# First modulation as rows, and the way in around it, in an adaLN block with random-feature attention and a routed feed-forward

## Chip, cores and metric

The kernel runs on one core of one Trainium2 chip. The metric is device time in microseconds (us) of one execution. All data is fp32.

## What is computed

Inputs: x (2 x 2048 x 256), a conditioning vector c (2 x 256), weights. With `_layernorm` over the 256 channels:

```python
mod = (_silu(L0_c) @ L0_wmod).reshape(2, 6, 1, 256)
sa, ca, ga, sb, cb, gb = mod[:, 0], ..., mod[:, 5]
ga = sign(ga) * max(|ga|, 0.25);  gb = sign(gb) * max(|gb|, 0.25)
h = _layernorm(x) * (1 + ca) + sa
x = x + ga * attn(h)
h = _layernorm(x) * (1 + cb) + sb
x = x + gb * ffn(h)
```

In `attn`, q, k and v come from `h @ W_attn + b_attn` with 16 heads of 16 channels; q and k are scaled by 1/4 and become 128 positive features each, `exp(x @ omega - |x|^2 / 2) / sqrt(128)`; the causal output is a running sum over keys, divided by its own normaliser, then projected. `ffn` routes each token to 2 of 4 experts that share Wi and Wo and differ by a rank-4 term. The change touches only the first modulation (sa and ca), the first layer norm's way to the attention, and the bias of q and k for the first block of tokens.

## The kernel before

**Tiling.** Each batch's 2048 tokens are cut into 4 blocks of 512, so there are 8 blocks; a block has 4 chunks of 128 tokens. Channels are split into KC = 2 halves of 128 partitions. Heads go in NG = 4 groups of HG = 4. Odd chunks are kept with their tokens reversed. The main loop runs over 8 blocks and 8 pairs of (group, two chunks), and interleaves with a block's attention the way in of the next block and the feed-forward of the ones before. At its end `keep_written_order` ties each engine's instructions to the order in which the program writes them, so each engine works its list in that order and waits only for data. The same holds for the queues: SyncE (SP) and ScalarE (ACT) each issue their DMAs in written order.

**The way in** is what runs once, before the main loop, to have block 0's features ready (lines 906 to 941, and the loads and constants from line 122 on):

- SP loads c (`ct_sb`, L122) and block 0's x in four pieces (L99). ScalarE issues the loads of `wm[0]` and `wm[1]` (the columns of wmod for sa and ca, L131), computes exp(-c) into `sig` (L135), then issues the loads of the q and k bias `bqk` (L136) and of the key and query columns of `w_sb` (L138). VectorE finishes silu(c) as `cs` (L140 to L142). SP goes on with omega (L144), the value columns (L145), the value bias (L146) and block 1's x.
- `warm(n, bank)` (L213) multiplies the identity by itself n times into a bank that nobody reads. WARM gives the counts, here 6 and 4.
- `ln_halves` (L306) computes mean and variance of the four chunks on VectorE and, by halves, the inverse root on GpSimd (L315).
- `columns(0)` (L245) computes the modulation as columns: for each of four groups of 128 outputs and each half k, the wm block is the stationary operand (128x128) and `cs`, two columns wide, is streamed. VectorE copies the result to `modT` and adds one into `scale1` (L252, L253).
- `norm1(0)` (L321) writes the normalised x, `xh`, on VectorE; `second_columns` (L171 to L175) prepares two small constants; `weights_twice` (L414) copies w_sb's query and key columns into a doubled layout `wd` on GpSimd.
- `channels1(0)` calls `to_channels`: for each half k, four transposes (L331) into one bank, then two evictions on VectorE (L342), for the even chunks and the reversed odd chunks, which apply scale1 and modT and write `hT`.
- `bias_twice` (L406, L408) doubles the bias; `twice_product` (L422) makes the doubled q and k, `pd`; VectorE adds the bias (L429), ScalarE and VectorE square every second row (L433, L441), and `features` (L476) multiplies by omega.

PSUM tiles come from rings: four banks for `mm_tile`, two for `side_tile`, and two fixed banks `pa`.

Of the kernel before, what the change touches and what calls it, by code (L numbers as in the profile page):

```python
# [9 lines left out]
FP = mybir.dt.float32  # L10
AF = mybir.ActivationFunctionType
ALU = mybir.AluOpType
AX = mybir.AxisListType

P = 128
# [17 lines left out]
def kernel(  # L33
# [18 lines left out]
    nc = tc.nc  # L52
    B, T, C = x.shape
    KC = C // P
# [6 lines left out]
    TB = 512  # L61
    NT = TB // P
# [5 lines left out]
    CG = P // 4  # L68


    W0, RHO = ER, ER + 1
    WARM = (6, 4)
    TH = TB // 2
    RG = 4
    assert M == P and KC == 2 and C == NH * DH and ER + 2 <= HW and RG * HW == P
# [1 line left out]
    const = ctx.enter_context(tc.tile_pool(name="const", bufs=1))  # L77
    work = ctx.enter_context(tc.tile_pool(name="work", bufs=2))
# [5 lines left out]
    def mm_tile(name):  # L84
        return psum.tile([P, TB], FP, tag="mm", name=name)
# [5 lines left out]
    st = {}  # L91
# [11 lines left out]
    w_sb = const.tile([P, KC, 3 * C], FP, name="w_sb")  # L103
# [3 lines left out]
    bqk = const.tile([P, 4], FP, name="bqk")  # L107
# [9 lines left out]
    modT = const.tile([P, 12, B], FP, name="modT")  # L117
    scale1 = const.tile([P, 2, KC, B], FP, name="scale1")
# [6 lines left out]
    wm = []  # L125
# [3 lines left out]
    wav = w_attn.rearrange("(k p) n -> p k n", p=P)  # L129
# [2 lines left out]

    cs = const.tile([P, KC, B], FP, name="cs")
    sig = const.tile([P, KC, B], FP, name="sig")
    nc.scalar.activation(sig, ct_sb, AF.Exp, scale=-1.0)  # L135
    nc.scalar.dma_start(bqk, b_attn[0 : 2 * C].rearrange("(c p) -> p c", p=P))  # L136
    for n in (1, 0):
        nc.scalar.dma_start(w_sb[:, :, n * C : (n + 1) * C], wav[:, :, n * C : (n + 1) * C])  # L138
    nc.vector.memset(om, -0.5)
    nc.vector.tensor_scalar_add(sig, sig, 1.0)  # L140
    nc.vector.reciprocal(sig, sig)
    nc.vector.tensor_mul(cs, ct_sb, sig)  # L142
    for j in range(HG):
        nc.sync.dma_start(om[2 * DH * j : 2 * DH * j + DH, :], omega)  # L144
    nc.sync.dma_start(w_sb[:, :, 2 * C : 3 * C], wav[:, :, 2 * C : 3 * C])  # L145
# [3 lines left out]
    ident = const.tile([P, P], FP, name="ident")  # L149
# [10 lines left out]
    def halves(ap):  # L160
        return ap.rearrange("p (j s d) -> p j s d", s=2, d=DH)
# [6 lines left out]
    def second_columns():  # L168

        second_row = work.tile([P, P], FP, tag="kt", name="second_row", bufs=1)  # L170
        nc.vector.memset(halves(second_row[:])[:, :, 0, :], 0.0)  # L171
        nc.vector.memset(halves(second_row[:])[:, :, 1, :], 1.0)
        nc.vector.tensor_mul(second_row, second_row, ident)
        nc.vector.tensor_reduce(on_second[:, 0:1], second_row, AX.X, ALU.add)
        nc.vector.tensor_scalar(on_second[:, 1:2], on_second[:, 0:1], -1.0, 1.0, ALU.mult, ALU.add)  # L175
# [6 lines left out]
    pa = [psum.tile([P, TB], FP, tag=f"pa{n}", name=f"pa{n}", bufs=1) for n in range(2)]  # L182
# [27 lines left out]
    def warm(n, bank):  # L210

        for _ in range(n):
            nc.tensor.matmul(bank[:, 0:P], ident, ident, start=True, stop=True)  # L213
# [25 lines left out]
    def columns(which):  # L239

        pm = mm_tile(f"pm{which}")
        pmv = pm[:, 0 : 4 * B].rearrange("p (n b) -> p n b", b=B)
        for n in range(4):
            for k in range(KC):
                nc.tensor.matmul(  # L245
                    pmv[:, n, :],
                    wm[3 * which + n // 2][:, k, (n % 2) * P : (n % 2 + 1) * P],
                    cs[:, k, :],
                    start=(k == 0),
                    stop=(k == KC - 1),  # L250
                )
        nc.vector.tensor_copy(modT[:, 6 * which : 6 * which + 4, :], pmv)  # L252
        nc.vector.tensor_scalar_add(  # L253
            scale1[:, which], modT[:, 6 * which + 2 : 6 * which + 4, :], 1.0
        )

    def gate(b, gi):

        pg = mm_tile(f"pg{b}_{gi}")
        for k in range(KC):  # L260
            nc.tensor.matmul(
                pg[:, 0:C], csb[b][:, k, :], wm[2 + 3 * gi][:, k, :],
                start=(k == 0), stop=(k == KC - 1),
            )
        gt2 = work.tile([P, 2, C], FP, tag="rho", name=f"gate{b}_{gi}", bufs=1)
        sgn, row = gt2[:, 0, :], gt2[:, 1, :]
        nc.vector.tensor_scalar(sgn, pg[:, 0:C], 0.0, 2.0, ALU.is_ge, ALU.mult)
        nc.vector.tensor_scalar_add(sgn, sgn, -1.0)
        nc.vector.tensor_mul(row, pg[:, 0:C], sgn)
        nc.vector.scalar_tensor_tensor(row, row, 0.25, sgn, ALU.max, ALU.mult)  # L270
        if gi == 0:
            nc.vector.tensor_mul(
                wp_g[b], wp_g[b], row.unsqueeze(1).to_broadcast([P, KC, C])
            )
            nc.vector.tensor_mul(bp_g[b], bp_g[b], row)
        else:
            rows_g[b] = row
# [18 lines left out]
    def ln_chunk(src, stats, mv, t):  # L296
        nc.vector.bn_stats(stats[:, t, :], src[:, t, :])
        nc.vector.bn_aggr(mv[:, t, :], stats[:, t, :])
# [4 lines left out]
        nc.gpsimd.tensor_tensor(rstd, rstd, mhalf, ALU.pow)  # L303
        return mv, rstd

    def ln_halves(src, nm):  # L306

        stats = work.tile([P, NT, 6], FP, tag="stats", name=f"stats{nm}")
        mv = work.tile([P, NT, 2], FP, tag="mv", name=f"mv{nm}")
        rstd = work.tile([P, NT], FP, tag="rstd", name=f"rstd{nm}")  # L310
        for h in (slice(0, 2), slice(2, 4)):
            for t in range(h.start, h.stop):
                ln_chunk(src, stats, mv, t)
            nc.vector.tensor_scalar_add(rstd[:, h], mv[:, h, 1], LN_EPS)
            nc.gpsimd.tensor_tensor(rstd[:, h], rstd[:, h], mhalf[:, h], ALU.pow)  # L315
        return mv, rstd

    def ln_apply(src, mv, rstd, nm):
        xh = work.tile([P, NT, C], FP, tag="xh", name=f"xh{nm}", bufs=1)
        for t in range(NT):  # L320
            nc.vector.tensor_scalar(  # L321
                xh[:, t, :], src[:, t, :], mv[:, t, 0:1], rstd[:, t : t + 1],
                ALU.subtract, ALU.mult,
            )
        return xh

    def to_channels(src, dst, b, which, nm, tiles):
        for k in range(KC):
            pt = tiles[k](f"pt{nm}_{k}")
            for t in range(NT):  # L330
                nc.tensor.transpose(  # L331
                    pt[:, t * P : (t + 1) * P], src[:, t, k * P : (k + 1) * P], ident
                )

            parts = ((0, 1), (1, -1)) if which == 0 else ((None, 1),)
            for odd, step in parts:
                out, ins = (
                    ap if odd is None else
                    ap.rearrange("p (a o u) -> p a o u", o=2, u=P)[:, :, odd, :]
                    for ap in (dst[:, k, :], pt[:])  # L340
                )
                nc.vector.tensor_scalar(  # L342
                    out if step > 0 else out[:, :, ::-1], ins,
                    scale1[:, which, k, b : b + 1],
                    modT[:, 6 * which + k, b : b + 1],
                    ALU.mult, ALU.add,
                )
# [15 lines left out]
    def norm1(i):  # L363
        s = st[i]
        s["xh"] = ln_apply(s["x"], *s["ln"], f"a{i}")
# [8 lines left out]
    def channels1(i, *tiles):  # L374
        s = st[i]
        s["hT"] = work.tile([P, KC, TB], FP, tag="hT", name=f"hT{i}", bufs=1)
        to_channels(s["xh"], s["hT"], i // NBLK, 0, f"a{i}", tiles or (side_tile, side_tile))
        s["feat"], s["qd"] = {}, {}
# [24 lines left out]
    def bias_twice():  # L403
        pb = mm_tile("pb")
        for g in range(2):
            nc.tensor.matmul(pb[:, 4 * g : 4 * g + 4], dup[:, g, :], bqk, start=True, stop=True)  # L406
        st["bias"] = const.tile([P, 2, 4], FP, name="bias_twice")
        nc.vector.tensor_copy(st["bias"], pb[:, 0:8].rearrange("p (g n) -> p g n", n=4))  # L408

    def weights_twice(g, side, tag):  # L410
        wd = work.tile([P, KC, P], FP, tag=tag, name=f"wd{g}{side}", bufs=2 if tag == "y" else 1)
# [283 lines left out]
    def norm2(i):  # L695
        st[i]["xh"] = ln_apply(st[i]["x"], *st[i]["ln"], f"f{i}")
# [207 lines left out]


    warm(WARM[0], pa[0])
    st[0]["ln"] = ln_halves(st[0]["x"], "a0")
    columns(0)
    warm(WARM[1], pa[1])
    norm1(0)  # L910
    second_columns()
    for g, side, tag in ((0, 1, "y"), (0, 0, "y"), (1, 1, "lT0"), (1, 0, "lT1")):
        weights_twice(g, side, tag)
    channels1(0)
    bias_twice()
    twice_product(0, 1, "qs", mm_tile)
    twice_product(0, 0, "qs", mm_tile)
    squares_under(0, 1)
# [172 lines left out]
    for i in range(N):  # L1091
        for k in range(PAIRS):
            n = (i * PAIRS + k) * 2
            g, t = k // 2, 2 * (k % 2)
# [46 lines left out]
    p, q = N - 1, N - 2  # L1141
# [97 lines left out]
```

## Time and profile before

| | us |
|---|---|
| three runs | 757.05, 759.88, 760.32 (median 759.88) |
| the profiled execution | 756.79 |
| its span, first to last instruction | 755.0 |
| first TensorE instruction (L213) | 1.43 |
| `columns(0)`, 16 instructions (L245) | 4.46 to 8.04 |
| first instruction of pd (L422) | 12.08 |
| first exp of the main work (L487) | 19.03 |

A matmul of fp32 data stands as two instructions in the profile, a transpose as one. PE is TensorE's matmuls, PEld its weight loads, DVE is VectorE, ACT ScalarE, POOL GpSimd, SP SyncE. In the timeline a row gives the start and the length in us, the engine, the line, what is written and read, the shapes, how many instructions were merged, and in brackets how long the engine had been idle and what ended it. In the chain of waits, each piece is what the last instruction of the span had to wait for, followed back; it gives the start, the length and the work.

### The profile page before, as it was taken

Reading aid. Unit: us, or ns where it says so; the run is one execution under the profiler, and the core shown is the slowest. Engines: PE = TensorE matmul, PEld = TensorE weight load, DVE = VectorE, ACT = ScalarE, POOL = GpSimd, SP = SyncE. Lnnn points to the kernel's source line nnn. Section 1 sums busy time; section 2 is a strip of 40 time slices with the busy share of each in tenths; the row PEclk is TensorE's granted clock in tenths of the full one; section 3 lists DMA queues with packets and bytes.
Section 4 is the critical chain, followed back from the end, with each engine's and each line's share of the span. In section 5 each row is a group of like instructions: output and inputs, shape, how many; then the busy total and the mean of one; then the engine's idle time right before and its main releaser. Section 6 shows DMA issues by size and latency. Waiting matters only on the chain.

```text
span 755.0 us, 24542 instructions
## 1 busy us (share of the span) xinstructions
PE 744.8 (99%) x10720; PEld 552.1 (73%) x10720; DVE 407.0 (54%) x1133; ACT 329.6 (44%) x742; POOL 148.3 (20%) x192
## 2 busy tenths in 40 slices
PE   9999999999999999999999999999999999999998
PEld 6667776666787767776787677877688777777776
DVE  5667667564663547534656456645364424654612
ACT  1665546535544444435544455435454343521010
POOL 3000322222210322011220122103130112005122
PEclk9999999999999999999999999999999999999999
DMA  4369443123301433023420342204240130002000
GB/s 134 111 195 298 146 143 100 44 82 120 114 29 32 129 112 114 17 72 119 124 72 33 111 125 82 67 29 130 73 127 16 50 110 17 16 34 83 1 29 28
DMA packets 44234, 65.46 MB, mean 87 GB/s; under 512 B 6752, under 2 KB 20256, under 8 KB 44128
## 3 DMA queue, kind: packets, MB, share of 16 engines
q1 hardware_dynamic: 42240, 62.33, 26.1%
q8 instruction: 84, 1.38, 0.8%
q10 hardware_dynamic: 1888, 1.58, 0.7%
q14 instruction: 22, 0.18, 0.1%
HBM read 35.32 MB, written 28.57 MB: 85 GB/s over the span
## 4 chain that ended last, share of the span: by engine, by line
PE 93%; DVE 4%; ACT 1%; issue 1%; DMA 0%; POOL 0%; DVEq 0%
PE ph L836 13%; PE pf L874 12%; PE pa L552 9%; PE pp L476 9%; PE pq L384 7%; PE ph L821 4%; PE pk L500 4%; PE pv L457 4%; PE py L621 4%; PE py L576 4%; PE py L627 3%; PE po L682 3%; PE pt L597 3%; PE pf L896 2%; PE ph L522 2%; PE pta L331 1%
## 5 line engine op out<-in xcount | busy, mean ns | idle before, releaser
L865 POOL TENSOR_TENSOR g<-g,r 128x256 f32<-128x256 f32 x128 | 90.6, 741 | 416.3 <-DVE r L864 416.3
L487 ACT ACTIVATE phi<-pp,lnm 128x512 f32<-128x512 f32 x256 | 155.2, 689 | 9.7 <-PE pp L476 3.6
L874 PE MATMUL pf<-wo_g,g 128*128 128x256 f32 x448 | 103.6, 382 | 0.4 <-ACT phi L487 0.2
L836 PE MATMUL ph<-h,wi_sb 128*128 128x256 f32 x448 | 101.9, 380 | 0.1
L836 PEld LDWEIGHTS ph<-h,wi_sb 128*128 128x128 f32 x448 | 84.3, 190 | 12.5 <-DVE r L864 0.5
L874 PEld LDWEIGHTS pf<-wo_g,g 128*128 128x128 f32 x448 | 82.6, 190 | 13.7 <-issue 2.2
L552 PEld LDWEIGHTS pa<-phi,phi 128*32 128x32 f32 x4096 | 77.5, 110 | 14.8 <-issue 13.3
L552 PE MATMUL pa<-phi,phi 128*32 128x128 f32 (+3 forms) x4096 | 85.4, 235 | 0.1
L850 ACT ACTIVATE g<-ph 128x256 f32<-128x256 f32 x112 | 33.9, 389 | 115.1 <-PE ph L821 115.1
L635 ACT COPY y<-py 128x128 f32<-128x128 f32 x128 | 27.8, 269 | 125.2 <-DVE ds L588 123.4
L561 DVE TENSOR_TENSOR am<-pa,causal 128x512 f32<-128x512 f32 x128 | 81.8, 681 | 0.0
L391 DVE TENSOR_SCALAR qs<-pq,bqk 128x512 f32<-128x512 f32 x30 | 22.5, 751 | 99.3 <-PE pq L384 94.6
L476 PE MATMUL pp<-f,om 32*128 32x512 f32 x512 | 73.6, 640 | 0.0
L542 ACT COPY kt<-pk 128x512 f32<-128x512 f32 x82 | 44.5, 594 | 54.8 <-PE pk L500 54.7
L864 DVE SCALAR_TENSOR_TENSOR r<-ph,rho 128x256 f32<-128x256 f32 x112 | 41.7, 422 | 45.6 <-PE ph L821 23.2
L384 PE MATMUL pq<-hT,w_sb 128*128 128x512 f32 x120 | 58.5, 612 | 0.0
L588 DVE COPY ds<-py 128x256 f32<-128x256 f32 (+1 forms) x63 | 25.7, 407 | 52.6 <-PE py L627 47.0
L621 PE MATMUL py<-am,v 128*32 128x128 f32 x1024 | 51.4, 273 | 0.0
L627 PE MATMUL py<-phi,S 128*32 128x128 f32 x960 | 50.1, 273 | 0.0
L597 PEld LDWEIGHTS pt<-ident,ds 128*128 128x128 f32 x120 | 12.8, 140 | 44.6 <-DVE ds L588 38.7
L500 PE MATMUL pk<-ident,phi 128*128 128x128 f32 x328 | 44.9, 275 | 0.5 <-ACT phi L487 0.4
L500 PEld LDWEIGHTS pk<-ident,phi 128*128 128x128 f32 x328 | 37.7, 141 | 7.1 <-ACT phi L487 3.0
(159 smaller groups left out, 968.2 us busy)
## 6 DMA issues: line engine op xcount, KB each, us to landing
f<-qd SPq DMA_DIRECT2D x60, 256.0 KB
qd<-qs SPq DMA_DIRECT2D x58, 256.0 KB
ydr<-y SPq DMA_DIRECT2D x32, 256.0 KB
num<-ydr SPq DMA_DIRECT2D x16, 256.0 KB
inv<-rdr SPq DMA_DIRECT2D x16, 256.0 KB
xt<-in_x_dram SPq DMA_DIRECT2D x7, 512.0 KB
out_dram<-xt SPq DMA_DIRECT2D x7, 512.0 KB
wo_g<-in_woT_dram SPq DMA_DIRECT2D x2, 1024.0 KB
```

Of the source, the lines that this page charges most:

```text
L384: nc.tensor.matmul(pq, w_sb[:, k, n * P : (n + 1) * P], s["hT"][:, k, :], start=(k == 0), stop=(k == KC - 1),)
L476: nc.tensor.matmul(pp, om[rs, :], f[rs, :], start=True, stop=True, tile_position=(2 * DH * j, 0))
L487: nc.scalar.activation(ph, pps[j], AF.Exp, bias=lnm)
L500: nc.tensor.transpose(pk[:, j * P : (j + 1) * P], phi[i, g, 1, j][:, t * P : (t + 1) * P], ident)
L542: nc.scalar.copy(kt.rearrange("p h m -> p (h m)"), turned[i, g, t])
L552: nc.tensor.matmul(pa[t % 2][c * CG : (c + 1) * CG, j * P + q0 : j * P + q1], phi[i, g, 1, j][:, t0 + c * CG : t0 + (c + 1) * CG], phi[i, ...
L561: nc.vector.tensor_mul(am, pa[t % 2][:].rearrange("p (h q) -> p h q", h=HG), causal[t % 2][:].unsqueeze(1).to_broadcast([P, HG, P]),)
L621: nc.tensor.matmul(py[rows[j], :], v[:, t, g * HG + j, :], am[:, j, :], start=True, stop=state is None,)
L627: nc.tensor.matmul(py[rows[j], :], state[:, rows[j]], phi[i, g, 0, j][:, tok], start=False, stop=True,)
L836: nc.tensor.matmul(ph, wi_sb[:, k, f * P : (f + 1) * P], s["h2"][:, k, ts], start=(k == 0), stop=False, skip_group_check=True,)
L865: nc.gpsimd.tensor_add(g, g, r)
L874: nc.tensor.matmul(po, s["g"][f][:, t * P : (t + 1) * P], wo_g[i // NBLK][:, f, :], start=(f == 0), stop=(f == NF - 1), skip_group_check=True,
```

## The change

The modulation for sa and ca is computed as rows: silu(c), repeated to 32 columns (`cs_rows`), is the stationary operand, the wm blocks are streamed 128 columns at a time into four groups of 32 partitions, ScalarE copies the result to SBUF, one transpose makes columns of it, and ScalarE writes modT and scale1 from there. `ln_halves` takes two functions that are called after its two halves, and the modulation, identity products and `bias_twice` stand there; the bias copy moves to ScalarE. The first block's transposes go chunk by chunk into four banks, and two of the four evictions are ScalarE's. `second_columns` moves behind them. There are four runs of identity products (7, 5, 8, 4) where there were two (6, 4). ScalarE issues the key columns' load before its exp, and bqk's load goes to SP, ahead of omega.

```diff
-    WARM = (6, 4)
+    WARM = (7, 5, 8, 4)
...
+    nc.scalar.dma_start(w_sb[:, :, C : 2 * C], wav[:, :, C : 2 * C])
     nc.scalar.activation(sig, ct_sb, AF.Exp, scale=-1.0)
-    nc.scalar.dma_start(bqk, b_attn[0 : 2 * C].rearrange("(c p) -> p c", p=P))
-    for n in (1, 0):
-        nc.scalar.dma_start(w_sb[:, :, n * C : (n + 1) * C], wav[:, :, n * C : (n + 1) * C])
+    nc.scalar.dma_start(w_sb[:, :, 0:C], wav[:, :, 0:C])
...
     nc.vector.tensor_mul(cs, ct_sb, sig)
+    cs_rows = const.tile([P, KC, CG // B, B], FP, name="cs_rows")
+    nc.vector.tensor_copy(cs_rows, cs[:].unsqueeze(2).to_broadcast([P, KC, CG // B, B]))
+    nc.sync.dma_start(bqk, b_attn[0 : 2 * C].rearrange("(c p) -> p c", p=P))
...
+    def modulation_rows():
+        pm = mm_tile("pm0")
+        for k in range(KC):
+            for n in range(4):
+                nc.tensor.matmul(
+                    pm[n * CG : (n + 1) * CG, 0:P], cs_rows[:, k].rearrange("p r b -> p (r b)"),
+                    wm[n // 2][:, k, (n % 2) * P : (n % 2 + 1) * P],
+                    start=(k == 0), stop=(k == KC - 1),
+                )
+        rows = work.tile([P, P], FP, tag="lT0", name="pm_rows", bufs=1)
+        nc.scalar.copy(rows, pm[:, 0:P])
+        return rows
+
+    def modulation_columns(rows):
+        pm = mm_tile("pm0T")
+        nc.tensor.transpose(pm[:, 0:P], rows, ident)
+        ins = pm[:, 0:P].rearrange("p (n c) -> p n c", c=CG)[:, :, 0:B]
+        nc.scalar.copy(modT[:, 0:2, :], ins[:, 0:2])
+        nc.scalar.activation(scale1[:, 0], ins[:, 2:4], AF.Identity, bias=1.0)
...
-    def ln_halves(src, nm):
+    def ln_halves(src, nm, between):
...
+            between.pop(0)()
...
+    def first_channels():
+        s = st[0]
+        s["hT"] = work.tile([P, KC, TB], FP, tag="hT", name="hT0", bufs=1)
+        s["feat"], s["qd"] = {}, {}
+        pts = [
+            [tile(f"pta0_{k}_{odd}") for k in range(KC)]
+            for odd, tile in enumerate((side_tile, mm_tile))
+        ]
+        for t in range(NT):
+            for k in range(KC):
+                nc.tensor.transpose(
+                    pts[t % 2][k][:, t // 2 * P : (t // 2 + 1) * P],
+                    s["xh"][:, t, k * P : (k + 1) * P], ident,
+                )
+        for odd in range(2):
+            for k in range(KC):
+                ins = pts[odd][k][:, 0 : NT // 2 * P].rearrange("p (a u) -> p a u", u=P)
+                out = s["hT"][:, k, :].rearrange("p (a o u) -> p a o u", o=2, u=P)[:, :, odd, :]
+                out = out[:, :, ::-1] if odd else out
+                scale, shift = scale1[:, 0, k, 0:1], modT[:, k, 0:1]
+                if k == 0:
+                    nc.vector.tensor_scalar(out, ins, scale, shift, ALU.mult, ALU.add)
+                else:
+                    nc.scalar.activation(out, ins, AF.Identity, scale=scale, bias=shift)
...
-        nc.vector.tensor_copy(st["bias"], pb[:, 0:8].rearrange("p (g n) -> p g n", n=4))
+        nc.scalar.copy(st["bias"], pb[:, 0:8].rearrange("p (g n) -> p g n", n=4))
...
     warm(WARM[0], pa[0])
-    st[0]["ln"] = ln_halves(st[0]["x"], "a0")
-    columns(0)
-    warm(WARM[1], pa[1])
+    rows = []
+
+    def rows_between():
+        rows.append(modulation_rows())
+        warm(WARM[1], pa[1])
+
+    def columns_between():
+        modulation_columns(rows[0])
+        bias_twice()
+        warm(WARM[2], pa[1])
+
+    st[0]["ln"] = ln_halves(st[0]["x"], "a0", [rows_between, columns_between])
     norm1(0)
-    second_columns()
     for g, side, tag in ((0, 1, "y"), (0, 0, "y"), (1, 1, "lT0"), (1, 0, "lT1")):
         weights_twice(g, side, tag)
-    channels1(0)
-    bias_twice()
+    first_channels()
+    warm(WARM[3], pa[1])
+    second_columns()
     twice_product(0, 1, "qs", mm_tile)
```

## The prediction, made before the change was run

> **What bounds the kernel now.** I read the page first, then the chain of waits over the first 20 us, then the same products later in the run, then VectorE's and GpSimd's timelines of the way in.
>
> The page (engines' busy time, and the chain by engine):
>
> ```profile
> span 755.0 us, 24542 instructions
> PE 744.8 (99%) x10720; PEld 552.1 (73%) x10720; DVE 407.0 (54%) x1133; ACT 329.6 (44%) x742; POOL 148.3 (20%) x192
> ...
> PE 93%; DVE 4%; ACT 1%; issue 1%; DMA 0%; POOL 0%; DVEq 0%
> ```
>
> TensorE is busy from 1.43 us to the end and carries 93% of the chain. The change touches only what runs before about 13 us. So its worth is by how much earlier, or later, the first line that it leaves alone starts on TensorE: the products pd of L422. All behind them stands in the same order on every engine. The chain of the way in (start us, us, what):
>
> ```profile
> 4.46 3.58 PE pm L245 x16
> 8.04 1.92 PE pa L213 x8
> 9.95 1.71 PE pta L331 x8
> 11.66 0.57 PE pb L406 x4
> 12.22 5.25 PE pd L422 x12
> ```
>
> It is TensorE without a gap from the first modulation to pd. A warm() product and a modulation product are two instructions each, a transpose is one; all move at one pitch: 3.58 / 16 = 0.22, 1.92 / 8 = 0.24, 1.71 / 8 = 0.21 us. Now the chain later, for the second modulation and for block 1's transposes:
>
> ```profile
> 44.02 1.04 PE pta L331 x8
> ```
>
> ```profile
> 74.54 1.68 PE pm L245 x16
> ```
>
> Here the same instructions take 0.105 and 0.13 us. So TensorE runs the way in at half its later speed. The view of windows gives a granted clock of 1.00 there too, so the rows are read instead. The full speed is there within pd: its 512-column instructions are 5.25 / 12 = 0.44 us from 12.22 on. I put the step at 12.0. What came before it: identity products from 1.43 to 4.37 (2.9 us) did not bring it; 2-column products from 4.46 on did not either; identity products from 7.90, then transposes, did, 4.1 us after they began. VectorE beside it:
>
> ```profile
> 8.07 0.17 DVE L252 COPY modT<-pm 128x8 f32<-128x8 f32 x1 [0.28 <-PE pm L245]
> 8.27 0.17 DVE L253 TENSOR_SCALAR scale<-modT 128x4 f32<-128x4 f32 x1
> 8.35 1.38 DVE L321 TENSOR_SCALAR xha<-xt,mva,rstda 128x256 f32<-128x256 f32 x4
> ...
> 10.84 1.90 DVE L342 TENSOR_SCALAR hT<-pta,scale,modT 128x256 f32<-128x256 f32 x4
> ```
>
> and GpSimd:
>
> ```profile
> 7.87 0.70 POOL L315 TENSOR_TENSOR rstda<-rstda,mhalf 128x2 f32<-128x2 f32 x1 [0.56 <-DVE rstda L314]
> 8.88 0.68 POOL L414 COPY wd<-w_sb 128x128 f32<-128x128 f32 x2 [0.30 <-DMA w_sb<-in_w_attn_dram]
> 11.77 1.48 POOL L414 COPY wd<-w_sb 128x128 f32<-128x128 f32 x6 [2.21 <-DMA w_sb<-in_w_attn_dram]
> ```
>
> VectorE waits for pm before it normalises, and does all four evictions of hT alone, 0.45 us apart; GpSimd waits 2.2 us for the query columns of w_sb.
>
> **The change, part by part, along TensorE.** *Start of the modulation.* The third DMA issue ahead of ScalarE's exp costs the pitch of the two before it, 0.51 us; the table load (1.87 to 3.15) then ends at 3.67 instead of waiting idle until sig at 3.59: +0.1. cs_rows is one VectorE copy of 128x64, between the 0.16 of 128x8 (L408) and the 0.29 of 128x128 (L173): 0.2 with its gap. pm0 starts at 4.46 + 0.3 = 4.76. The warm-up before it, 14 instructions, ends at 1.81 + 13 x 0.213 = 4.58, so TensorE stays covered.
>
> *Modulation as rows.* 16 instructions, 32 columns of weights in four column groups, 128 columns moving. The nearest row is L576, of the same form: 0.46 us for 16 at full speed, so 0.9 at half. It needs both wm: the old line asked for wm1 at 6.19 without a wait, and the fourth omega load, which stood behind that landing, went out at 5.28. I take 5.5 as its end; if wm1 is last, 5.9.
>
> *When full speed comes.* This decides the rest and no row shows it. Now nothing thin lies between 1.43 and the transposes. Lower bound: 4.4, since 2.9 us of products were not enough. Nearest row: 4.1 us after a dense start, so 1.43 + 4.1 = 5.5. Upper bound: twice that stretch, 9.6. I take 5.5. The Trainium skill, TensorE: Matmul & The Clock Gate, Part 1, says that the clock doubles after one busy window of about 3.4 us which runs free of the kernel. By that rule the step would lie between 4.8 and 8.3 from one execution to another, and pd between 10.7 and 12.2; halved pitch and a step 4.1 us after the start agree with it here.
>
> *Ten identity products' instructions, the transpose, pb.* At 0.11 each the ten take 1.1: to 6.6; the row copy on ScalarE (0.27, L635) hides under them, and the cover is ample. Transpose 0.1. ScalarE's two small copies (0.2 each, by the 128x4 exp) are off the path. pb needs bqk, now on SP's queue behind four x loads, issued between 3.2 and 4.2. No row shows its landing; w_sb's, issued at 5.67, was consumed at 8.88, 3.2 later; so 6.4 to 7.4. TensorE idles 0 to 0.7, I take 0.4, and pb ends at 7.5. Behind bqk on SP stand omega, the value columns, bv_bc and block 1's x, each 0.4 to 1 us later; they are used at 17.4, 19.9, 23.9 and 33.9, so this costs nothing.
>
> *Sixteen more:* 16 x 0.11 = 1.8, to 9.3.
>
> *xh.* VectorE no longer waits 0.28 for pm nor makes modT and scale1 (0.34), but the third and fourth chunks need the second root, which ends at 8.57: 8.6 + 0.32 + 0.41 = 9.35 instead of 9.73. The w_sb columns issued at 1.9 instead of 5.7 now share the DMA engines with the last x loads (DMA share 0.90 in 4 to 6 us): the second bn_stats already waited 0.48 for x. Between 0 and 0.5 later, I take 0.2: xh ends at 9.55.
>
> *Transposes, evictions.* Six of the eight run before the fourth chunk is there; the last two end at 9.8. VectorE takes two evictions (0.45 apart, 0.54 the last) and ScalarE two (0.39 each, L850, which has the form): hT's first half-channel is complete at 9.9 + 0.54 = 10.45. The closing eight instructions, 0.9, end at 10.7. second_columns (1.0 us) now follows the evictions, to 11.6, and is needed by ScalarE only once z is out, 2.0 after pd starts: free, and 0.1 late at worst if pd came 1 us earlier. GpSimd's copies run 8.6 to 10.9 with w_sb there early; the first pair is done by 9.3. The wait for w_sb goes from a queue that TensorE didn't feel: nothing.
>
> *Sum.* pd starts at 10.75. Before, 12.08, with 0.08 lost in its first instruction at the old speed: 12.16. The gain is 1.4 us. It goes up to 1.7 (10.45, bound by the evictions), down to 0.4 for a step halfway to its upper bound, 7.6 (ten instructions to 7.7, pb to 8.2, sixteen to 10.0, transposes to 10.8, pd at 11.8), to nothing at 8.4, and at 9.6 it is a loss of 0.6 (pb to 8.9, sixteen to 11.0, transposes to 11.85, pd at 12.75).
>
> **Against the runs.** The profiled execution took 756.8 (span 755.0, 1.8 around it); it alone would become 755.4. The three runs are 757.05, 759.88, 760.32: with it two pairs 3.1 apart, and the profile shows only the lower one. I set the sum against the mean of the four, 758.5: **757.1**.
>
> **Rivals.**
> 1. *The clock doesn't come early* (slower). The 32-column products or the short idle at 4.6 could break the stretch, so that the step stays at 12.0. Then the added instructions count double: rows to 5.7, ten to 7.8, transpose and pb to 8.9, sixteen to 12.2, transposes to 13.1, pd at 14.0: 1.85 later, 760.4; with a step at 15.4, one 3.4 us later, 3.5 later. It decides from a step after 8.4 on. For it: 2.9 us did not bring it at first. Against: 32-column products fill the body at full speed (L552, 4096 of them). Chance 0.08.
> 2. *Input-bound.* w_sb and bqk come between the x loads; xh or pb is late by 1 us more, TensorE waits: gain 0.4, 758.1. For: DMA share 0.90, bqk's 4-byte pieces; against: x is issued before either. Chance 0.14.
> 3. *The upper pair is the clock.* In the runs near 760 the step may have come a stretch later, 15.4 instead of 12.0; pd's first 3.4 us at half speed lose 1.7. The early dense start removes that too: 1.4 + 1.7 = 3.1, 756.8 against the median of 759.9, or down to the profile's 755.4 if all of the upper pair is that. For: 3.1 between pairs, which nothing in the body's rows explains; against: 1.7 is not 3.1. Chance 0.16. The forecast keeps 0.62.
>
> **Numbers.** About 0.5% (3.8 us) can be told from no change. Faster by that means under 756.1 against the median: the forecast falls there if the changed runs are of the lower level (755.4), which I give 0.35 of its 0.62, plus 0.10 from the third rival: 0.33. Slower needs the first rival on the upper level: 0.04. The rest, 0.63, is the same. Range: 755.0 (lower level, 1.8 gained) to 760.0 (upper level, 0.3 gained); it leaves out part of rivals 1 and 3.
>
> **What would show it.** pm0's 16 instructions near 5 us in under 0.9; the identity products after them at 0.11 each; pta's first transpose by 9.4; pd before 11. Wrong: identity products at 0.21 up to 9 us or later, a wait for bqk over 1 us before pb, or pp's first omega wait.

## The result, and the profile after

| | before | changed |
|---|---|---|
| median of 22 runs, us | 758.69 | 757.65 |
| lowest, highest | 757.05, 761.36 | 755.94, 758.80 |
| profiled execution, span | 756.79, 755.0 | 756.65, 755.0 |

The ratio is 0.9978, 95% interval 0.9968 to 0.9987. The change gains 0.1% to 0.3%, within the 0.5% that counts as the same; the median moved by 1.04 us where 1.4 was forecast, and the time lies in the range. But the two profiled executions have the same span to 0.1 us, and the first product pd (now L474), which was to start 1.4 us earlier, starts where it did: 12.11, before 12.08. So the size came true and the path by which it was to come did not; that the two sizes agree is luck, as the last sections show. The page of the changed kernel:

```profile
span 755.0 us, 24604 instructions
PE 744.5 (99%) x10749; PEld 550.5 (73%) x10749; DVE 406.3 (54%) x1129; ACT 331.3 (44%) x748; POOL 148.3 (20%) x192
```

The chain of waits over its first 20 us (start us, us, what):

```profile
4.92 1.65 PE pm L264 x16
6.57 1.31 PE pa L215 x10
7.88 0.11 PE pm0T L276
7.99 0.43 PE pb L458 x4
8.42 1.89 PE pa L215 x16
10.31 0.67 PE pta L364 x6
10.98 0.98 DVE hT L375 x2
...
12.12 5.38 PE pd L474 x12
```

The modulation takes 1.65 us instead of 3.58, and the identity products behind it run at 0.11 to 0.13 us an instruction: the clock is up, in this execution from 6.44 us on. What was saved went into 26 instructions of identity products, 10 and 16, which end at 10.15; six transposes follow, then two evictions on VectorE. VectorE's own timeline shows why the products alone are not to blame:

```profile
5.87 0.43 DVE L321 BATCH_NORM_STATS2 statsa<-xt 128x6 f32<-128x256 f32 x1 [0.43 <-DMA xt<-in_x_dram]
...
6.97 0.43 DVE L321 BATCH_NORM_STATS2 statsa<-xt 128x6 f32<-128x256 f32 x1 [0.25 <-DMA xt<-in_x_dram]
...
9.29 0.73 DVE L346 TENSOR_SCALAR xha<-xt,mva,rstda 128x256 f32<-128x256 f32 x2 [0.27 <-POOL rstda L339]
10.97 1.00 DVE L375 TENSOR_SCALAR hT<-pta,scale,modT 128x256 f32<-128x256 f32 x2 [0.94 <-PE pta L364]
```

The third bn_stats (VectorE's statistics of one chunk of x) waits for x (6.97, before 6.42 without a wait), the second root comes late after it, and the last chunks of xh end at 10.02 instead of 9.73. Then VectorE itself waits 0.94 us for the transposes.

Each run also has its mean granted clock, the share of TensorE's full speed granted over its span, and the runs fall into groups by it. It counts speed that was taken away again, not the time before the first grant: the profiled run of before has 1.000, though its first 12 us ran at half speed. Before: 83 runs of three comparisons below (for the 22 of before in the table above no clock is on record); changed: the 22 and the 10 of `again`.

| mean clock | before: runs, median us | changed: runs, median us |
|---|---|---|
| 0.999 and 1.000 | 49 (59%), 757.58 | 18 (56%), 756.41 |
| 0.997 and 0.998 | 15 (18%), 758.84 | 14 (44%), 758.00 |
| 0.996 and less | 19 (23%), 759.38 | none |

One window of 3.41 us at half speed is 1.7 us, or 0.002 of the span: the middle row is one such window, the last row two or three. So two things are to be explained: 1.2 us between the groups at full clock, though pd starts at the same time, and a group that is gone.

### The profile page after: what moved, and what is told of

It is laid out like the page before. It is cut to its first block, busy times and chain, and to the rows that moved or that the text cites. A ratio compares the mean times of both kernels' runs of the same rounds, so it can differ in the third digit from the quotient of the medians.

```text
span 755.0 us, 24604 instructions
## 1 busy us (share of the span) xinstructions
PE 744.5 (99%) x10749; PEld 550.5 (73%) x10749; DVE 406.3 (54%) x1129; ACT 331.3 (44%) x748; POOL 148.3 (20%) x192
## 4 chain that ended last, share of the span: by engine, by line
PE 92%; DVE 5%; ACT 1%; DMA 1%; issue 1%; POOL 0%; SPq 0%; DVEq 0%
PE ph L888 13%; PE pf L926 12%; PE pa L604 9%; PE pp L528 8%; PE pq L436 7%; PE ph L873 4%; PE pk L552 4%; PE pv L509 4%; PE py L673 4%; PE py L628 3%; PE po L734 3%; PE py L679 3%; PE pt L649 3%; PE pf L948 2%; PE ph L574 2%; PE ptf L383 1%
```

## The experiments

**again**: the changed kernel once more.

> The changed kernel once more, for a second profile. Theory A (the clock's windows lie anywhere against the kernel's start; what the change wins is that full speed is there before pd in every execution, while before it came at 12.0 in the one profiled and later in others): the step lies somewhere between 4.2 and 7.6 us, pd starts between 11.3 and 12.4, the ratio to before is again near 0.998. Theory B (the clock has no part in the medians, the gain is in the transfers): the step may lie anywhere, and spans don't follow it.

Ratio 0.9984 (0.9971 to 0.9997). Here the clock came at 5.48, pd at 12.22, the span was 754.7. The step's place varies, within the bounds that A set, and the span did not follow it: pd was held by something else. TensorE also waited 0.38 us for bqk before pb in this execution. The gain itself is there again.

**warm4**: fewer identity products.

```diff
-    WARM = (7, 5, 8, 4)
+    WARM = (7, 5, 4, 4)
```

> Third run of identity products cut from 8 to 4 (WARM 7, 5, 4, 4). Theory A1 (in the changed kernel the sixteen instructions of the third run end at 10.15, after the first three chunks of xh, and hold the transposes up): the first transpose comes near 9.3, pd at 11.2 instead of 12.1, the time 0.9 us below the changed kernel. Theory A2 (pd waits for the last chunk of xh and four evictions whatever stands before): pd stays at 12.1, the time the same.

Ratio to before 0.9995 (0.9982 to 1.0008). The chain of its way in:

```profile
8.21 1.00 PE pa L215 x8
9.20 0.67 PE pta L364 x6
9.87 0.98 DVE hT L375 x2
...
11.02 2.37 PE pd L474 x5
```

A1 is right on the way in: pd starts at 11.00, 1.1 earlier (x came 0.4 earlier in this execution; in `warm4b` below, where it came only 0.1 earlier, pd starts 0.8 earlier). A1 is wrong on the time: the span is 755.7, 0.8 longer, and the median is 757.89 beside 756.82 for `again` in the same comparison. Set against the changed kernel instruction by instruction, TensorE is 1.1 us ahead until 132, has lost that by 134, and loses 0.7 more near 585. In the chain near 585:

```profile
585.34 0.20 PE py L679 x6
585.54 0.41 issue
585.95 0.27 PE py L679
```

TensorE stands still amid products whose data is there; the chain names nothing but "issue", time in which the engine waited for nothing that the profile shows. **warm4b** is the same kernel again:

> The kernel with WARM 7, 5, 4, 4 once more. In its first profile pd started at 11.0 but the span was 755.7, with TensorE idle 0.67 us at 132 and 0.41 us at 585 while nothing in the profile held it. Theory C (these idle times belong to this program's order of instructions, so the gain of the way in is given back in every execution): both come again within 2 us of the same places, span about 755.5, ratio to before near 1.000. Theory D (they fall anywhere): not at these places; with pd near 11.0 the span is about 754, and the ratio near 0.997.

Ratio 0.9991 (0.9977 to 1.0005), pd at 11.27, span 755.0. The same place in its chain:

```profile
584.89 0.20 PE py L679 x6
585.09 0.12 issue
585.21 0.27 PE py L679
```

It stops at the same instruction, and again at 132, but for 0.12 and 0.15 us instead of 0.41 and 0.67. So C is right on the places and wrong on the size: they belong to the program, their length to the execution. The same kind of gap stands at 317 us in the chains of two of three profiles of before (0.22, 0.49) and of `rows_only` (0.49), at 133 us in the same two of before (0.13, 0.41), and at neither place in the changed kernel's. All "issue" pieces of the chain, most of which every profile has, make 4.7, 5.2 and 5.8 us in three profiles of before, and 4.7 in both of the changed kernel.

No run was made to find what causes the gaps, but the traces show what they wait for. Every page has such a line among its DMA queues (loads, MB, share of the DMA engines' time); this is the changed kernel's:

```profile
q8 instruction: 84, 1.38, 0.8%
```

These are 84 loads of 16 KB for TensorE's some 21,600 instructions, one for every 256. The chains of the 14 traces hold 14 gaps of this kind, from 0.12 to 0.67 us (one of 0.12 near 314 us, which every trace has, is another kind). Each of the 14 comes when 193 instructions and a whole multiple of 256 have started, that is, always at the same point of a run of 256. TensorE goes on 1.2 to 1.5 us after the end of one of these loads, and at none of the 83 such points of each trace is it under 1.18. So, by these times, TensorE waits there for its own next instructions, where their load comes late. Which products stand at such a point depends on how many instructions stand before them. Near 133 and 317 us TensorE passes it 1.2 to 1.4 us after the load's end in all three profiles of before, and 3.6 or more after it in the two of the changed kernel. Why a load comes late at one point and not at another is open.

**nowarm**: no identity products at all (WARM = 0, 0, 0, 0).

> No identity products at all (WARM 0, 0, 0, 0). Theory A: nothing dense runs before pd, so full speed comes one or two windows of 3.4 us after pd starts; pd starts near 11.2 but its first 3.4 to 6.8 us run at half speed: 0.8 to 2.5 us slower than the changed kernel, so level with before or up to 1.5 us slower. Theory B: identity products only fill idle time: pd 0.9 us earlier and the time 0.9 us below the changed kernel.

Ratio 1.0026 (1.0002 to 1.0049): slower than before. Its chain:

```profile
9.08 1.45 PE pta L364 x5
...
10.63 0.99 DVE hT L375 x2
...
11.78 8.07 PE pd L474 x12
```

pd starts at 11.77, but its twelve instructions take 8.07 us instead of 5.38; full speed comes at 17.21. That is theory A, and B falls: the products pay for themselves through the clock. The median, 759.43, is 2.6 above that of `again` in the same comparison, a little past the 2.5 that A allowed; two of the ten runs, at 764.7, lost two windows besides (mean clock 0.996).

**thin**: two-column products back, all else as changed.

```diff
-        rows.append(modulation_rows())
+        columns(0)
...
-        modulation_columns(rows[0])
```

> The changed kernel with its first modulation as two-column products again (columns(0) in place of the rows and their transpose), all else kept. Theory A: the 3.5 us of two-column products break the dense stretch, so full speed comes after 11 us, the identity products cost 0.21 each, pd starts between 13.5 and 15: 1.5 to 3.5 us above the changed kernel, so slower than before. Theory B (the clock comes near 6.4 all the same): the products end near 7.5 instead of 6.5, pd 0 to 1 us later.

Ratio 1.0025 (1.0003 to 1.0046). Its windows of time (from and to, length, busy time and instructions of PE, PEld, DVE, ACT and POOL, granted clock, DMA share, GB/s):

```profile
4.62:8.03 3.41, 3.39 (x30) 3.23 (x29) 2.39 (x13) 0.00 (x0) 0.71 (x1) 1.00 0.86 258
8.03:11.44 3.41, 3.41 (x17) 3.41 (x17) 1.83 (x7) 0.17 (x1) 2.81 (x9) 0.50 0.74 171
11.44:14.86 3.42, 3.42 (x23) 2.66 (x22) 1.88 (x7) 1.02 (x2) 0.98 (x2) 1.00 0.28 98
```

Neither theory had this. The first identity products brought full speed at 4.62 already, and it was taken away for one window at 8.03, after a window of two-column products (1.75 us), identity products (1.2) and pb's four-column ones, though TensorE was busy for 3.39 of its 3.41 us. pd started at 13.57. So A is right that thin products cost the clock, and in this profile wrong on how: here they make it fall instead of keeping it from coming. It is the only profile of that state, and not of the usual one: of the ten runs it alone has a clock of 0.998, and its 758.75 lies below the median of 760.68. Two runs, at 756.6 and 756.8, are as fast as the changed kernel; the other seven, from 759.9 to 763.1, lost no window after the first grant. That their first grant came late, as A has it, fits their times and their clocks, but no profile shows it.

**keylate4**: warm4 with the key columns' load behind the exp, as before.

```diff
-    nc.scalar.dma_start(w_sb[:, :, C : 2 * C], wav[:, :, C : 2 * C])
     nc.scalar.activation(sig, ct_sb, AF.Exp, scale=-1.0)
+    nc.scalar.dma_start(w_sb[:, :, C : 2 * C], wav[:, :, C : 2 * C])
```

> WARM 7, 5, 4, 4 and the key columns' load put back behind ScalarE's exp. Theory E (that load, issued at 1.9, takes the DMA engines from x: the third and fourth bn_stats came 0.55 later than before): bn_stats at 5.7, 6.4 and 7.0 as before, xh complete near 9.4 instead of 10.0, pd near 10.8. Theory F (x lands at its own pace): bn_stats stay near 5.9, 7.0, 7.5 and pd at 11.0 or later, held by w_sb.

Ratio 0.9986 (0.9972 to 1.0001), so the time alone shows no gain. VectorE's timeline:

```profile
5.84 0.43 DVE L321 BATCH_NORM_STATS2 statsa<-xt 128x6 f32<-128x256 f32 x1 [0.47 <-DMA xt<-in_x_dram]
...
6.59 0.42 DVE L321 BATCH_NORM_STATS2 statsa<-xt 128x6 f32<-128x256 f32 x1
...
7.14 0.39 DVE L321 BATCH_NORM_STATS2 statsa<-xt 128x6 f32<-128x256 f32 x1
```

The third no longer waits for x, and the fourth follows it; xh is complete at 9.60, pd starts at 10.92. Over all profiles the fourth bn_stats starts at 7.57 in the mean of eight with the early load (7.11 to 7.85) and at 7.09 in six with the late one (6.93 to 7.17): the early load costs x 0.48 us in the mean, though single executions overlap (`warm4`, with the early load, has the 7.11). Theory E is right.

**rows_only**: the kernel before with the rows and their transpose in place of columns(0), nothing else.

```diff
-    columns(0)
+    modulation_columns(modulation_rows())
```

> The kernel before with the first modulation as rows and its transpose alone (old WARM 6, 4, old loads, old evictions). Theory A: TensorE then idles between the shorter modulation and xh, so the clock is granted late or taken away again in part of the executions; pd starts 0.5 to 1.3 earlier than before in the best case, the spread of the runs stays as wide as that of before (4 us), the ratio between 0.997 and 1.000. Rival: the rows alone carry the whole gain, ratio 0.998 or lower with the narrow spread of the changed kernel (under 3 us).

Ratio 0.9999 (0.9983 to 1.0014), runs from 756.2 to 760.5. pd at 11.65, 0.4 earlier, nothing left at the end: the rows alone don't carry the gain, which is theory A's side, though pd gained a little less than the least it allowed. Its profile caught a withdrawn window, from 611.5 to 614.9, in the middle of the kernel.

**oddsplit**: evictions shared by chunk.

```diff
-    WARM = (7, 5, 8, 4)
+    WARM = (7, 5, 4, 2)
...
-                if k == 0:
+                if odd == 0:
```

> WARM 7, 5, 4, 2 and the four evictions shared by chunk (VectorE the even chunks, ScalarE the odd ones) instead of by half of the channels. Theory G (pd waits for VectorE's two evictions of the first half in a row, 0.98 us on the chain): the first half is complete 0.25 to 0.45 earlier, pd near 10.7. Rival: xh's last chunk or the identity products hold pd, which stays at 11.0.

Ratio 0.9981 (0.9967 to 0.9995). x came late here and pd started at 11.20, so the start alone says little; from the last xh to pd it is 1.16 us, in warm4 1.44 and in warm4b 1.32. That is 0.2 to 0.3 us less, the low end of G. But the edit also takes out two of the closing identity products, which end the wait for pd in warm4b's chain, so what the evictions alone are worth is not separated. The chain now goes from GpSimd's root to seven of its copies of w_sb, which hold pd.

**before2, before3**: two more profiles of the kernel before.

> The kernel before, for another profile. Theory A (windows of 3.41 us that lie anywhere against the start): full speed comes at another time than 12.0, between 10.7 and 15.4, or comes early, near 4.5 to 5, and is taken away again while the two-column products run; a later step shows as pd instructions at 0.85 us and a later pp, at most 1.7 us later. Theory B (the clock's steps belong to the program): 12.0 again, pp at 17.4.

> As before2, a third profile of the kernel before: Theory A: a step at a third place, pp's start following it; Theory B: 12.0 again, pp at 17.4.

The clock came at 10.91 and 10.85, pd at 12.11 and 11.93, pp (the products with omega, behind pd) at 17.47 and 17.30. So the step moves, but the start of pd hardly does: with an earlier step, pd waits for evictions or for w_sb's query columns. A step later than 12.0 was not caught. before2 showed the withdrawn window:

```profile
608.25:611.66 3.41, 2.90 (x40) 1.83 (x43) 1.04 (x4) 1.21 (x4) 0.47 (x1) 1.00 0.47 158
611.66:615.07 3.41, 3.41 (x96) 3.37 (x84) 0.38 (x2) 0.00 (x0) 2.33 (x4) 0.50 0.10 34
615.07:618.48 3.41, 3.41 (x27) 2.22 (x20) 2.29 (x6) 2.48 (x6) 0.00 (x0) 1.00 0.01 2
```

The window before it holds 0.51 us of idle and mostly the 16-row low-rank products. Here is what its chain shows there:

```profile
608.66 0.72 PE ph L821 x8
609.39 0.39 ACT g L850
...
609.82 1.52 PE ph L821 x5
```

**fill**: three identity products into that wait, in the changed kernel.

```diff
-                 (unit, q, 1, (turn, side_tile, (1,)))),
+                 (unit, q, 1, (turn, side_tile, (1,)), (warm, 3, pa[1]))),
```

> The changed kernel with three identity products where TensorE waits 0.51 us near 609 us, between the two sets of 16-row products of L873. Theory H (the upper group of runs, near 758.0 with a mean clock of 0.998, is one window of 3.41 us at half speed that a window over this thin stretch brings on): the upper group goes or shrinks from 4 in 10 to under 1 in 10, the lower stays at 756.4, the ratio to before falls to 0.997 or lower. Rival (the half-speed window comes from elsewhere, the way in for one): the upper group stays at 4 in 10, ratio 0.998.

Ratio 0.9971 (0.9957 to 0.9984). All 12 runs lie between 756.08 and 757.46 with a clock of 0.999 or 1.000; without the fill 14 of 32 had lost a window. The timeline of its TensorE:

```profile
608.10 0.71 PE L873 MATMUL ph<-lT,lb_sb 16*128 16x256 f32 x8
608.75 0.94 PE L215 MATMUL pa<-ident 128*128 128x128 f32 x6
609.61 1.24 PE L873 MATMUL ph<-lT,lb_sb 16*128 16x256 f32 x8
```

The six instructions fill the wait, and the products behind it end at the same time as in the changed kernel. Theory H is right: with the fill, here and in the next kernel, none of 22 runs is in the middle group. It comes from this one place, which the change doesn't touch.

**both**: the fill, the late key load, evictions by chunk, WARM = 7, 5, 4, 2.

> The three identity products near 609 us, and a shorter way in: key columns' load behind the exp, evictions shared by chunk, WARM 7, 5, 4, 2. By theories E and G pd starts at 10.6 instead of 12.1; of these 1.5 us about half are left at the end, as in keylate4: the lower group at 755.7. With theory H the ratio to before is 0.996; without it 0.9975. Rival: idle TensorE behind pb lets the clock be withdrawn in part of the executions, ratio 0.998 and a spread over 3 us.

Ratio 0.9964 (0.9948 to 0.9979), median 755.99 beside 758.28; 10 of 10 runs without a withdrawn window; pd at 10.78. This version is faster than before, by 0.2% to 0.5%, and its median is the lowest of all. Its interval overlaps with that of `fill`, so the share of the way in is not settled by it. TensorE waited for its instructions here too, 0.41 us at 132 and 0.22 at 585. The way in now ends on GpSimd:

```profile
8.06 0.80 POOL rstda L339
8.86 1.88 POOL wd L466 x7
...
10.78 3.24 PE pd L474 x7
```

## Why the prediction was right, and where it was not

*Total.* 1.4 us forecast, 1.04 measured in the medians, 1.7 by the ratio. The sign, the range and the "same" hold. The sum's end point does not, and that the size came near is luck: in the profiled execution pd gained nothing, and what the medians gained came, as far as it is known, from lost windows and from waits for instructions, for which the sum has no term.

*The step that failed* is "pd starts at 10.75". It started at 12.11 and 12.22, and of the four signs named for it only the pitch of 0.11 came. Five of its terms were mis-sized. The rows end at 6.5, not 5.5: wm1 was last, which was priced at 5.9, and half speed lasted until 6.44 instead of 5.5. With that the sixteen instructions end at 10.15 instead of 9.3 and hold the transposes back, though bqk cost no wait here where 0.4 was set down; `warm4b` shows what eight of the sixteen cost there, 0.8 of pd's start. Behind the transposes two of VectorE's evictions stand in a row, 0.98, where the sum has the last alone, 0.54. The early key load delays x by 0.48 where 0.2 was taken. And ScalarE's evictions take 0.56 each, not 0.39: the row of L850, a plain Relu, was too cheap for an activation with scale and bias per partition; nothing waited for them here.

*"All behind them stands in the same order", hence gain in, gain out,* failed too. warm4 started pd 1.1 us earlier and ended 0.8 us later: TensorE's waits for its next instructions, at places that belong to the program's order of instructions, gave it back. The prediction had no term for it.

*The early clock* was right: 6.44 and 5.48 for a nearest row of 5.5 and bounds of 4.4 and 9.6. The lower bound's reason does not hold, though: in `both` 2.85 us of identity products, from 1.43, brought full speed at 4.28; the 2.9 us in before did not, and only 2.6 of them lay in the one window from 1.76 to 5.18. `nowarm` and `thin` show its price: pp starts 2.4 and 1.5 us later than in the changed kernel, and both end slower than before. The first rival named this mechanism, and in `thin` it took place: the clock is at half speed from 8.03 to 11.44, pd at 13.57 for 14.0 worked out. In the two profiles of the changed kernel it did not take place; in `rows_only`, with the same 32-column products but only the old identity products around them, full speed came at 10.78.

*The second rival* was half right: x comes late by the key load, by half of the 1 us that it asked for; and bqk comes late in some executions, by 0.38 us of waiting in `again`.

*The third rival* had the right kind and the wrong place: a window of the clock does make the upper group of runs, but near 609 us, in both kernels, and the change leaves it there. What the change took away is the group with two or three lost windows, 23% of before's runs; that this is the early clock withdrawn again over the two-column products, as in `thin`, is argued, not shown. What speaks for it: the 12 runs with two lost windows are only 1.0 us above the group at full clock, and the 7 with three only 2.3, where two and three windows in the middle of the kernel would cost 3.4 and 5.1. Windows lost in the way in, which runs at half speed in any case, would cost little.

*"The wait for w_sb goes from a queue that TensorE didn't feel"* holds for the profile it was read in. In before2 the wait for w_sb ends at 11.53, GpSimd's copies follow, and they release pd at 12.12.

*What stays open* is a part of the 1.2 us between the groups at full clock. From pd to the end it is 743.4 us in the mean of three profiles of before (with 1.7 for its lost window taken off `before2`) and 742.7 in three with the changed way in (the two and `fill`); pd starts 0.1 later in these. So the profiles show about 0.6, and in their chains 0.4 of it is waits for instructions. Three profiles a side, 1.0 us apart in before, are few for that. Steps of the clock later than 12.0 in before would give more; no profile caught one.

## What to carry to other kernels

A saving in the prologue of a kernel that one engine fills is worth only what is left after the next wait, and after the places where the engine waits for its own instructions, which shift with the program: measure the end, not the start. Where the clock follows what TensorE does, look for thin stretches (few columns streamed, few rows, a short wait) and lay identity products into a wait that is there anyway: six instructions in one wait of 0.5 us took a loss of 1.6 us out of 4 runs in 10. A single profile of such a kernel is one draw; the mean clock beside each run's time tells part of which draw it was, the windows taken away, but not a late first grant.

## What the runs showed of the hardware

- The clock is granted and withdrawn on a grid. Between the changes of the granted clock that the traces record there are 744.11, 747.52 and 600.75 us: 218, 219 and 176 times 3.4133. The first grant came at 6.44 and at 5.48 in two executions of the changed kernel. The Trainium skill, TensorE: Matmul & The Clock Gate, Part 1, gives windows of 3413 ns that run free of the kernel's start; the traces agree.
- It falls without an idle window. It was taken away after windows in which TensorE was busy 3.39 of 3.41 us (two-column products for half of it, `thin`) and 2.90 of 3.41 us (16-row products for most of it, before2). The Trainium skill, TensorE: Matmul & The Clock Gate, Part 1, has in its table that the cold state comes after at least one idle window of about 3.4 us. The measurement decides: in these two windows thin work did not count as full.
- Transposes count for the grant. In before2 the window from 7.50 to 10.91 brought full speed with identity products in 1.9 us of it and transposes in 1.0, in the first profile of before the window from 8.59 to 12.00 with 1.4 and 1.9; there the window from 1.76 to 5.18, with 2.6 us of identity products and two-column products behind them, did not. The Trainium skill, TensorE: Matmul & The Clock Gate, Part 4, says that transposes don't count as busy work in the same way; the measurement decides here too.
- TensorE can wait for its own instructions. They come in 84 loads of 16 KB; the 14 gaps of 0.12 to 0.67 us all stand at the same point of a run of 256 instructions, and TensorE goes on 1.2 to 1.5 us after a load's end.
